# Agent attention: agents' scores laid out with pixels on partitions, half an image at a time, and two steps put on GpSimd

## The chip, the cores and the metric

The kernel runs on one core of one Trainium2 chip. The metric is the device time of one execution in microseconds (us); the median of three runs is quoted. Next to it stands one profiled execution, from which all durations of single instructions come.

## What is computed

The program is four residual layers, each `x = x + layer(groupnorm(x))`, on images of 32 x 192 x 56 x 56 in float32. The change touches layer 0 alone, an attention through 49 agents per head, six heads of 32 channels. Cut to what matters:

```python
qkv = xf @ Wqkv + bqkv                       # n = 3136 pixels, c = 192
agent = q averaged over 8 x 8 pixels         # A = 49 agents
agent_attn = softmax(ah * scale @ kh.T + pos_bias, axis=-1)    # over pixels
agent_v = agent_attn @ vh
q_attn = softmax(qh * scale @ ah.T + agent_bias, axis=-1)      # over agents
out = q_attn @ agent_v + depthwise3x3(v)
out = out @ proj_w + proj_b
```

The first softmax (the agents') has one row per head and agent, 294 rows of 3136 pixels. The second (the pixels') has one row of 49 for each pixel and head.

## The kernel before, in words

`attention` takes the 32 images one after the other (loop at line 833). An image is cut into four strips of columns, 16, 16, 16 and 8 wide (`WIDTHS`), each with its 56 rows in two halves; a strip holds 8 or 4 blocks of 112 pixels (`SUB`), 28 blocks in an image. `PAIR` is 98, two heads of 49 agents; `HA` is 294, all heads' agents. The keys and queries are never formed: `seen` (line 582 on) multiplies the agents into the weights, so that scores come straight from the normalised pixels `xs_a` and `xs_c` (which also carries the biases).

Agents' softmax, strip by strip. `weigh` (lines 651 to 667) makes scores with the agents on partitions: for each of three pairs of heads two halves of up to 448 pixels, each from two matmuls (lines 659, 660). VectorE finds the negated maximum straight from PSUM (line 661), ScalarE takes the exponential and the row's sum together (line 663). `turn` (line 682 on) transposes the weights on TensorE (line 691) so that pixels lie on partitions, ScalarE copies them to `prT` (line 694), and `gather` multiplies them with the transposed values (line 706). `settle` transposes the result back and adds two halves (lines 715 to 719). `join` (line 721 on) brings the four strips with their own maxima and sums together and gives `values`.

Pixels' softmax. `ask` (line 743 on) makes scores with pixels on partitions, 294 columns for each block (lines 751, 752), two blocks to a PSUM tile; VectorE finds the maximum of each head and subtracts it (lines 755, 756), ScalarE takes the exponential of four blocks (line 764), VectorE sums, inverts and multiplies (lines 766 to 768). `turn_back` transposes (line 778), `answer` multiplies with `values` and adds onto the convolution's result `o` (lines 791 to 797), `project` applies the last matrix and adds onto the image (lines 806 to 819).

Beside these stand the depthwise convolution of the values, `convolve` (eight multiply-adds on VectorE for each of two tiles, line 646; strip j needs the values of strip j + 1, which `find_v` makes), and `moments` (lines 507 to 536), the statistics and 8 x 8 sums of the next image.

The order. The program is written in a dataflow framework: it decides ahead of the run in which order each engine goes through its instructions, led by the order of writing and by what it reckons to be ready, and it puts in the waits. On the chip every engine then goes through its own list strictly in order. So the order of the calls in the loop (lines 841 to 887) is what one shapes. In the part before the loop over `t`, the four strips of the agents' softmax are written with the convolutions of the next strip between them; `moments` comes last, and `ask(0)` stands ahead of `join`. In the loop over `t` strips are asked, turned back, projected and answered in a staggered manner, and the next image's agents, values and first convolution are put between.

Buffers. All matmuls share four PSUM tiles of two banks (tag `ps`). `pr` and `pqT` share five SBUF buffers (tag `weights`), `prT` and `pq` two (tag `turned`).

## Time and profile before

| | us |
|---|---|
| median of 3 runs | 10793.86 (10781.03 to 10796.38) |
| the profiled execution | 10811.08 |
| its span, first to last instruction | 10809.3 |
| first agents' copy `gq_a` starts | 198.3 |
| last agents' copy `gq_a` starts | 4862.3 |
| TensorE clock granted, mean | 0.950 |

The attention is the first 45 per cent or so of the span; the scan of layer 1 follows, and the last part from about 8,370 us on does layers 2 and 3.

How to read the profile. PE is TensorE's matmuls and PEld its weight loads, DVE is VectorE, ACT ScalarE, POOL GpSimd, SP the engine that issues DMAs. A float32 matmul appears as two matmul instructions; a transpose as one. A line for a group of instructions gives: source line, engine, operation, what is written and read by the program's names, sizes as partitions x elements, the count; then busy us and mean ns of one; then how long the engine stood idle just before, and what ended that. A line for a stretch gives its bounds, its length, and then busy us of PE, PEld, DVE, ACT and POOL with the number of instructions, the granted clock and the DMA share. A line in order of time gives start, length, engine and instruction. The ends of matmuls are modelled: where matmuls follow each other, the distance of their starts is the price.

### The profile page before, as it was taken

The numbers are of one execution on the slowest core, as the hardware profiler recorded it, in microseconds if no ns is written. First come the engines' busy times: TensorE is split into PE (matmuls) and PEld (weight loads), VectorE is DVE, ScalarE is ACT, GpSimd is POOL, SyncE is SP. The second block draws the span as 40 slices with busy tenths as digits, with TensorE's granted clock in tenths as the row PEclk, the third lists the DMA queues.
The fourth block names the chain that finished last, engine by engine and source line by source line (L and its number), as shares of the span: only waits on it lengthen the run. The fifth ranks groups of instructions, "written<-read, shape, count | busy, mean of one in ns | idle before, by whom it ended". The sixth has DMA issues, their size and how long they took to land. (4 is left out here: it accounts for less than half of the span.)

```text
span 10809.3 us, 166766 instructions
## 1 busy us (share of the span) xinstructions
PE 9604.3 (89%) x64806; PEld 5959.0 (55%) x64806; DVE 9260.0 (86%) x11668; ACT 6372.8 (59%) x11964; POOL 2918.0 (27%) x2614
## 2 busy tenths in 40 slices
PE   6999999999999999998888888888888799999998
PEld 3555555555555555554333333333333577787876
DVE  5888888888888888887999999999999577777877
ACT  3555555555555555554666666666666466666766
POOL 0000000000000000002655555555555444444441
PEclk8999999999999999998999999999999899999999
DMA  4211221112121111111344333333444589999998
GB/s 122 63 47 49 63 64 63 37 58 63 64 63 35 61 46 46 46 34 56 92 102 98 97 97 97 97 97 97 97 101 103 153 269 273 274 275 273 278 274 264
DMA packets 1104877, 1240.31 MB, mean 115 GB/s; under 512 B 773091, under 2 KB 807200, under 8 KB 1091992
## 3 DMA queue, kind: packets, MB, share of 16 engines
q1 hardware_dynamic: 1083148, 1201.53, 38.8%
q10 hardware_dynamic: 20932, 28.02, 1.0%
q8 instruction: 516, 8.45, 0.3%
q14 instruction: 281, 2.30, 0.1%
HBM read 915.94 MB, written 306.43 MB: 113 GB/s over the span
## 5 line engine op out<-in xcount | busy, mean ns | idle before, releaser
L646 DVE SCALAR_TENSOR_TENSOR o<-v_a,att_w,o 128x896 f32<-128x896 f32 (+1 forms) x1024 | 1053.3, 1029 | 421.7 <-ACT v_a L620 296.6
L1163 POOL MEMSET f<- 128x1 f32 x96 | 8.8, 98 | 4842.7 <-DMA st_c<-st 4837.7
L1543 DVE STREAM_TRANSPOSE z<-turned 128x1792 f32<-128x1792 f32 x192 | 677.4, 3528 | 258.3 <-ACT turned L1543 257.8
L1543 ACT COPY y<-ps 64x252 f32<-64x252 f32 (+1 forms) x2304 | 784.0, 340 | 157.9 <-PE ps L1543 128.1
L1156 ACT ACTIVATE q<-q 128x784 f32<-128x784 f32 x384 | 328.3, 855 | 813.6 <-DVE q L1151 638.5
L663 ACT ACTIVATE pr<-ps,low 98x896 f32<-98x896 f32 (+1 forms) x384 | 352.3, 918 | 567.8 <-DVE low L661 567.8
L911 PE MATMUL ps<-sq,fixed 128*128 128x392 f32 x512 | 296.8, 742 | 427.7 <-ACT sq L1234 427.7
L764 ACT ACTIVATE pq<-pq 112x1176 f32<-112x1176 f32 x224 | 265.3, 1184 | 683.3 <-DVE pq L756 654.1
L751 PE MATMUL ps<-gq_a,xs_a 128*112 128x294 f32 x1792 | 609.0, 422 | 46.6 <-DVE pq L756 24.1
L1543 POOL TENSOR_TENSOR xn<-x,scale 128x896 f32<-128x896 f32 x192 | 328.4, 1711 | 1192.3 <-DMA x<-x 759.4
L646 DVE SCALAR_TENSOR_TENSOR o<-v_c,att_w,o 128x448 f32<-128x448 f32 (+1 forms) x1024 | 634.3, 619 | 7.5 <-ACT v_c L631 2.4
L659 PE MATMUL ps<-xs_a,gk_a 128*98 128x448 f32 (+1 forms) x1536 | 638.9, 497 | 0.0
L660 PE MATMUL ps<-xs_c,gk_c 125*98 125x448 f32 (+1 forms) x1536 | 631.3, 492 | 0.0
L911 PE MATMUL ps<-x,weights 128*128 128x392 f32 x1536 | 573.7, 516 | 31.1 <-DVE bv L1185 14.1
L752 PE MATMUL ps<-gq_c,xs_c 125*112 125x294 f32 x1792 | 581.4, 411 | 0.0
L1543 PEld LDWEIGHTS ps<-toep,y 128*32 128x32 f32 x16896 | 508.2, 151 | 113.4 <-ACT y L1543 109.2
L1543 PE MATMUL ps<-toep,y 128*32 128x112 f32 x16896 | 554.8, 287 | 0.0
L1543 PE MATMUL ps<-rows,xn 128*112 128x112 f32 x3072 | 378.5, 281 | 159.6 <-POOL xn L1543 136.0
L1543 ACT ACTIVATE turned<-ps,rs 128x448 f32<-128x448 f32 (+1 forms) x576 | 384.4, 668 | 203.4 <-PE ps L1543 195.7
L1543 PE MATMUL ps<-fixed,padded 128*128 128x168 f32 x3072 | 490.0, 314 | 0.0
L766 DVE TENSOR_REDUCE sm<-pq 112x24 f32<-112x1176 f32 x224 | 307.7, 1374 | 181.9 <-ACT pq L764 181.9
L1543 PEld LDWEIGHTS ps<-fixed,padded 128*128 128x128 f32 x3072 | 455.6, 195 | 2.4 <-issue 1.9
(367 smaller groups left out, 25548.6 us busy)
## 6 DMA issues: line engine op xcount, KB each, us to landing
toep<-spans SPq DMA_DIRECT2D x192, 2352.0 KB
x<-x SPq DMA_DIRECT2D x576, 392.0 KB
x<-x SPq DMA_DIRECT2D x896, 196.0 KB
out_x<-done SPq DMA_DIRECT2D x384, 196.0 KB
spans<-lags SPq DMA_DIRECT2D x24, 2352.0 KB
x<-in_x SPq DMA_DIRECT2D x32, 1568.0 KB
x<-x SPq DMA_DIRECT2D x32, 1568.0 KB
x<-in_x SPq DMA_DIRECT2D x64, 392.0 KB
```

Source lines behind the costliest of these rows:

```text
L646: nc.vector.scalar_tensor_tensor(dst, tap(i), dww[:, t, i : i + 1], dst, ALU.mult, ALU.add)
L659: mm(ps[P2, h, :n], g[:, cols], xs_a[j][:, px], start=True, stop=False)
L660: mm(ps[P2, h, :n], gk_c[0:KC, 2 * j + h, cols], xs_c[j][0:KC, px], start=False, stop=True)
L663: nc.scalar.activation(pr[:, :, :n], ps[P2, :, :n], AF.Exp, bias=low[:, j, p : p + 1], accum_out=sums[:, j, p : p + 1])
L751: mm(ps[:SUB, i, :HA], xs_a[j][:, px], g, start=True, stop=False)
L752: mm(ps[:SUB, i, :HA], xs_c[j][0:KC, px], gq_c[0:KC, 2 * j + (q + i) // ns], start=False, stop=True)
L764: nc.scalar.activation(flat, flat, AF.Exp)
L766: nc.vector.tensor_reduce(sm, rows, AX.X, ALU.add)
L911: mm(out, aa, srcs[t][h], start=True, stop=False)
L1156: nc.scalar.activation(den, den, AF.Ln)
L1163: nc.gpsimd.memset(s, 0.0)
L1543: return lambda *args, **kw: self.tc.keep_in_program_order(do(*args, **kw))
```

## The change

- `weigh` and `turn` go. `score` makes the agents' scores with pixels on partitions, in the form that `ask` has, and ScalarE copies them from PSUM to SBUF (`sc`, up to 8 blocks of 294).
- The softmax is kept for half images: strips 0 and 1, then strips 2 and 3. `highest` takes the maximum over the blocks on VectorE; `top` transposes these maxima, takes the maximum over the pixels and spreads the negated result over a diagonal matrix (`apart`); `lower` multiplies that with ones, which gives the row of maxima on all partitions, adds it to the scores on VectorE and takes the exponential on ScalarE. All are in place.
- `fold` adds the blocks up on GpSimd, and `add_up` finishes the sums with TensorE. `gather` and `settle` run once for each half image, and `join` has two parts to bring together in place of four.
- In `ask` the last product moves from VectorE to GpSimd.
- The block buffers become three of 8 blocks and one of 4. The tag `weights` has three buffers in place of five and also holds `by_x`, `tops`, `side` and `halves`. Some small tiles lose their second buffer.
- The calls of an image are written in a new order up to `join`; the loop over `t` stays.

```diff
--- before.py
+++ after.py
@@ -454,6 +454,7 @@
     mm = nc.tensor.matmul
     UP, LOW = slice(0, 64), slice(64, 128)
     HALVES = ((0, UP), (1, LOW))
+    WB = 3
...
@@ -473,6 +474,8 @@
     gk_c, gq_c, xs_c = ready.gk_c, ready.gq_c, ready.xs_c
 
     NK = len(WIDTHS)
+    ones = cp.tile([128, SUB], F32, name="ones", tag="ones")
+    nc.gpsimd.memset(ones, 1.0)
     xs_a = [cp.tile([128, S * w], F32, name=f"xs_a{j}", tag=f"xs_a{j}") for j, w in enumerate(WIDTHS)]
...
@@ -516,7 +519,7 @@
         nc.vector.bn_aggr(mv[:, 0], st_a.rearrange("p a b -> p (a b)"))
         nc.vector.bn_aggr(mv[:, 1], st_c.rearrange("p a b -> p (a b)"))
         pool_a, pool_c = small("pool_a", [128, AG]), small("pool_c", [65, AG])
-        by_x = [wp.tile([128, n, POOL], F32, name="by_x", tag=f"by_x{n}", bufs=1) for n in (S, S // 2)]
+        by_x = [wp.tile([128, n, POOL], F32, name="by_x", tag="weights", bufs=WB) for n in (S, S // 2)]
...
@@ -586,7 +589,7 @@
             n = (128, 65)[i]
             mm(ps[:n, i, : 4 * AG], w[0][:, cols], ag[0], start=True, stop=True)
             mm(ps[:n, i, 4 * AG : HA], w[1][:, cols], ag[1], start=True, stop=True)
-        g = small(name, [128, HA])
+        g = sp.tile([128, HA], F32, name=name, tag=name, bufs=1)
...
@@ -648,23 +651,74 @@
         return o
 
 
-    def weigh(j, g, low, sums):
-        _, n, _ = sizes(j)
-        prs = []
+    def blocks(j, name):
+        n = 2 * sizes(j)[2]
+        return wp.tile([SUB, n, HA], F32, name=name, tag=f"turned{n}", bufs=n // 4 + n // 8)
+
+    def score(j, g):
+
+        _, _, ns = sizes(j)
+        sc = blocks(j, "sc")
+        for q in range(0, 2 * ns, 2):
+            ps = psum()
+            for i in range(2):
+                px = slice((q + i) * SUB, (q + i + 1) * SUB)
+                mm(ps[:SUB, i, :HA], xs_a[j][:, px], g, start=True, stop=False)
+                mm(ps[:SUB, i, :HA], xs_c[j][0:KC, px], gk_c[0:KC, 2 * j + (q + i) // ns], start=False, stop=True)
+            nc.scalar.copy(sc[:, q : q + 2], ps[:SUB, :, :HA])
+        return sc
+
+    def highest(parts):
+
+        tops = wp.tile([SUB, 2, HA], F32, name="tops", tag="weights", bufs=WB)
+        for i, (j, sc) in enumerate(parts):
+            n = 2 * sizes(j)[2]
+            nc.vector.tensor_reduce(tops[:, i], sc[:, :n].rearrange("p q c -> p c q"), AX.X, ALU.max)
+        nc.vector.tensor_tensor(tops[:, 0], tops[:, 0], tops[:, 1], ALU.max)
+        return tops
+
+    def fold(parts):
+
+        (_, a), (j, b) = parts
+        side = wp.tile([SUB, 2, HA], F32, name="side", tag="weights", bufs=WB)
+        rest = [(t, q) for t, n in ((a, 8), (b, 2 * sizes(j)[2])) for q in range(0, n, 2)]
+        (t, q), (u, r) = rest[:2]
+        nc.gpsimd.tensor_tensor(side[:, 0:2], t[:, q : q + 2], u[:, r : r + 2], ALU.add)
+        for t, q in rest[2:]:
+            nc.gpsimd.tensor_tensor(side[:, 0:2], side[:, 0:2], t[:, q : q + 2], ALU.add)
+        nc.gpsimd.tensor_tensor(side[:, 0], side[:, 0], side[:, 1], ALU.add)
+        return side
+
+    def top(i, side, low):
+
+        ps = psum()
         for p in range(3):
-            cols = slice(p * PAIR, (p + 1) * PAIR)
-            ps = psum()
-            for h in range(2):
-                px = slice(h * n, (h + 1) * n)
-                mm(ps[P2, h, :n], g[:, cols], xs_a[j][:, px], start=True, stop=False)
-                mm(ps[P2, h, :n], gk_c[0:KC, 2 * j + h, cols], xs_c[j][0:KC, px], start=False, stop=True)
-            nc.vector.tensor_reduce(low[:, j, p : p + 1], ps[P2, :, :n], AX.XY, ALU.max, negate=True)
-            pr = wp.tile([PAIR, 2, CH], F32, name="pr", tag="weights", bufs=5)
-            nc.scalar.activation(
-                pr[:, :, :n], ps[P2, :, :n], AF.Exp, bias=low[:, j, p : p + 1], accum_out=sums[:, j, p : p + 1]
+            nc.tensor.transpose(ps[P2, 0, p * SUB : (p + 1) * SUB], side[:, 0, p * PAIR : (p + 1) * PAIR], ident[:SUB, :SUB])
+        nc.vector.tensor_reduce(
+            low[:, i], ps[P2, 0, : 3 * SUB].rearrange("p (a n) -> p a n", a=3), AX.X, ALU.max, negate=True
+        )
+        apart = sp.tile([PAIR, 3, PAIR], F32, name="apart", tag="apart", bufs=1)
+        nc.vector.tensor_tensor(
+            apart, ident[P2, P2].unsqueeze(1).to_broadcast([PAIR, 3, PAIR]), _bc(low[:, i], [PAIR, 3, PAIR]), ALU.mult
+        )
+        return apart
+
+    def lower(parts, apart):
+        ps = psum()
+        mm(ps[:SUB, 0, :HA], ones[P2, :SUB], apart.rearrange("p a b -> p (a b)"), start=True, stop=True)
+        for j, sc in parts:
+            n = 2 * sizes(j)[2]
+            nc.vector.tensor_tensor(
+                sc[:, :n], sc[:, :n], ps[:SUB, 0, :HA].unsqueeze(1).to_broadcast([SUB, n, HA]), ALU.add
             )
-            prs.append(pr)
-        return prs
+            flat = sc[:, :n].rearrange("p q c -> p (q c)")
+            nc.scalar.activation(flat, flat, AF.Exp)
+
+    def add_up(i, side, sums):
+        ps = psum()
+        for p in range(3):
+            mm(ps[P2, 0, p : p + 1], side[:, 0, p * PAIR : (p + 1) * PAIR], ones[:SUB, 0:1], start=True, stop=True)
+        nc.vector.tensor_copy(sums[:, i], ps[P2, 0, 0:3])
 
     def turn_v(j, v):
 
@@ -679,32 +733,20 @@
             nc.scalar.copy(vT[:, s0 : s0 + 2], ps[:SUB, :, : 3 * 128])
         return vT
 
-    def turn(j, prs):
-
-        _, _, ns = sizes(j)
-        prT = wp.tile([SUB, 8, HA], F32, name="prT", tag="turned", bufs=2)
-        for q in range(0, 2 * ns, 2):
-            ps = psum()
-            for i in range(2):
-                h, s = divmod(q + i, ns)
-                for p in range(3):
-                    nc.tensor.transpose(
-                        ps[:SUB, i, p * PAIR : (p + 1) * PAIR], prs[p][:, h, s * SUB : (s + 1) * SUB], ident[P2, P2]
-                    )
-            nc.scalar.copy(prT[:, q : q + 2], ps[:SUB, :, :HA])
-        return prT
-
-    def gather(j, prT, vT):
-
-        _, _, ns = sizes(j)
+    def gather(parts):
+
         ps = psum()
+        steps = [(s, sizes(j)[2], sc, vT) for j, sc, vT in parts for s in range(sizes(j)[2])]
         for p in range(3):
             cols = slice(p * PAIR, (p + 1) * PAIR)
-            for s in range(ns):
+            for k, (s, ns, sc, vT) in enumerate(steps):
                 for h, r in HALVES:
                     c = h * 128 + p * 64 if p < 2 else 256 + h * 64
-                    mm(ps[r, 0, cols], vT[:, s, c : c + 64], prT[:, h * ns + s, cols], start=(s == 0), stop=(s == ns - 1))
-        halves = wp.tile([128, HA], F32, name="halves", tag="halves", bufs=1)
+                    mm(
+                        ps[r, 0, cols], vT[:, s, c : c + 64], sc[:, h * ns + s, cols],
+                        start=(k == 0), stop=(k == len(steps) - 1),
+                    )
+        halves = wp.tile([128, HA], F32, name="halves", tag="weights", bufs=WB)
         nc.scalar.copy(halves, ps[:, 0, :HA])
         return halves
 
@@ -722,17 +764,17 @@
 
         m = small("m", [PAIR, 3])
         nc.vector.tensor_reduce(m, low.rearrange("p j a -> p a j"), AX.X, ALU.min)
-        f = small("f", [PAIR, NK, 3])
-        nc.vector.tensor_tensor(f, m.unsqueeze(1).to_broadcast([PAIR, NK, 3]), low, ALU.subtract)
+        f = small("f", [PAIR, 2, 3])
+        nc.vector.tensor_tensor(f, m.unsqueeze(1).to_broadcast([PAIR, 2, 3]), low, ALU.subtract)
         nc.scalar.activation(f, f, AF.Exp)
         nc.vector.tensor_tensor(sums, sums, f, ALU.mult)
         den = small("den", [PAIR, 3])
         nc.vector.tensor_reduce(den, sums.rearrange("p j a -> p a j"), AX.X, ALU.add)
         nc.vector.reciprocal(den, den)
-        nc.vector.tensor_tensor(f, f, den.unsqueeze(1).to_broadcast([PAIR, NK, 3]), ALU.mult)
+        nc.vector.tensor_tensor(f, f, den.unsqueeze(1).to_broadcast([PAIR, 2, 3]), ALU.mult)
         by_pair = got.rearrange("p j (a d) -> p (j a) d", a=3)
         nc.vector.tensor_tensor(
-            by_pair, by_pair, _bc(f.rearrange("p j a -> p (j a)"), [PAIR, NK * 3, 2 * HD]), ALU.mult
+            by_pair, by_pair, _bc(f.rearrange("p j a -> p (j a)"), [PAIR, 2 * 3, 2 * HD]), ALU.mult
         )
...
@@ -742,7 +784,7 @@
 
     def ask(j, g):
         _, _, ns = sizes(j)
-        pq = wp.tile([SUB, 8, HA], F32, name="pq", tag="turned", bufs=2)
+        pq = blocks(j, "pq")
...
@@ -765,7 +807,7 @@
             sm = sp.tile([SUB, 4 * HEADS], F32, name="sm", tag="sm", bufs=4)
             nc.vector.tensor_reduce(sm, rows, AX.X, ALU.add)
             nc.vector.reciprocal(sm, sm)
-            nc.vector.tensor_tensor(rows, rows, _bc(sm, [SUB, 4 * HEADS, AG]), ALU.mult)
+            nc.gpsimd.tensor_tensor(rows, rows, _bc(sm, [SUB, 4 * HEADS, AG]), ALU.mult)
...
@@ -778,7 +820,7 @@
                 nc.tensor.transpose(
                     ps[P2, h, s * SUB : (s + 1) * SUB], pq[:, q, p * PAIR : (p + 1) * PAIR], ident[:SUB, :SUB]
                 )
-            t = wp.tile([PAIR, 2, CH], F32, name="pqT", tag="weights", bufs=5)
+            t = wp.tile([PAIR, 2, CH], F32, name="pqT", tag="weights", bufs=WB)
             nc.scalar.copy(t[:, :, :n], ps[P2, :, :n])
...
@@ -828,35 +870,47 @@
     gk = seen(ag, wkT, gk_c, "gk_a")
     for j in range(NK):
         normed(nxt, rs, nb, j)
-    v, o = {0: find_v(0), 1: find_v(1)}, {}
-    o[0] = convolve(0)
+    v = {0: find_v(0), 1: find_v(1)}
+    o = {0: convolve(0)}
     for b in range(NB):
         x, more = nxt, b + 1 < NB
         if more:
             nxt = ready.image(nc, a, b + 1)
         beside(b)
-        low, sums = small("low", [PAIR, NK, 3]), small("sums", [PAIR, NK, 3])
-        got = sp.tile([PAIR, NK, C], F32, name="got", tag="got", bufs=1)
-        turned, asked, back = {}, {}, {}
-        for j in range(NK):
-            prs = weigh(j, gk, low, sums)
-            if j == 0:
-                gq = seen(ag, wqT, gq_c, "gq_a")
-            vT = turn_v(j, v[j])
-            if j > 0:
-                halves = gather(j - 1, *turned[j - 1])
-            if j + 2 < NK:
-                v[j + 2] = find_v(j + 2)
-            turned[j] = turn(j, prs), vT
-            if j > 0:
-                settle(j - 1, halves, got)
-            if j + 1 < NK:
-                o[j + 1] = convolve(j + 1)
-            elif more:
-                mv, pools = moments(nxt)
-        halves = gather(NK - 1, *turned[NK - 1])
+        low, sums = small("low", [PAIR, 2, 3]), small("sums", [PAIR, 2, 3])
+        got = sp.tile([PAIR, 2, C], F32, name="got", tag="got", bufs=1)
+        asked, back, sc, vT = {}, {}, {}, {}
+        sc[0] = score(0, gk)
+        gq = seen(ag, wqT, gq_c, "gq_a")
+        sc[1] = score(1, gk)
+        tops = highest([(j, sc[j]) for j in range(2)])
+        for j in range(2):
+            vT[j] = turn_v(j, v[j])
+        v[2] = find_v(2)
+        o[1] = convolve(1)
+        apart = top(0, tops, low)
+        sc[2] = score(2, gk)
+        lower([(j, sc[j]) for j in range(2)], apart)
+        v[3] = find_v(3)
+        o[2] = convolve(2)
+        sc[3] = score(3, gk)
+        side = fold([(j, sc[j]) for j in range(2)])
+        halves = gather([(j, sc[j], vT[j]) for j in range(2)])
+        add_up(0, side, sums)
+        tops = highest([(j, sc[j]) for j in range(2, 4)])
+        for j in range(2, 4):
+            vT[j] = turn_v(j, v[j])
+        settle(0, halves, got)
+        o[3] = convolve(3)
+        apart = top(1, tops, low)
         asked[0] = ask(0, gq)
-        settle(NK - 1, halves, got)
+        lower([(j, sc[j]) for j in range(2, 4)], apart)
+        if more:
+            mv, pools = moments(nxt)
+        side = fold([(j, sc[j]) for j in range(2, 4)])
+        halves = gather([(j, sc[j], vT[j]) for j in range(2, 4)])
+        add_up(1, side, sums)
+        settle(1, halves, got)
         values = join(low, sums, got)
         done, o = o, {}
         st = small("st", [128, 2, 9])
```

More of the change, by code (lines that the diff above doesn't have):

```diff
@@ L526, in moments @@
         )
-        fours = small("fours", [64, 2 * POOL, POOL])
+        fours = sp.tile([64, 2 * POOL, POOL], F32, name="fours", tag="fours", bufs=1)
         for h, r in HALVES:
```

## The prediction

> **What bounds the kernel now.** I read the page first (busy shares, slices), then the stretches of one image, then the groups of instructions in it, then single instructions in order of time.
>
> ```profile
> PE 9604.3 (89%) x64806; PEld 5959.0 (55%) x64806; DVE 9260.0 (86%) x11668; ACT 6372.8 (59%) x11964; POOL 2918.0 (27%) x2614
> ...
> PE   6999999999999999998888888888888799999998
> ...
> DVE  5888888888888888887999999999999577777877
> ...
> POOL 0000000000000000002655555555555444444441
> ```
>
> The change touches only the attention, slices 1 to 18 (to about 5,000 us). There GpSimd is idle, TensorE full and VectorE close to it. The copy of gq_a starts at 198.3 us in the first of the 32 images and at 4862.3 in the last: 150.5 us an image. Three stretches of one image (busy us of each engine follow the length):
>
> ```profile
> 2006.00:2070.00 64.00, 63.39 (x444) 40.91 (x443) 57.72 (x85) 36.54 (x74) 0.00 (x0) 1.00 0.37 124
> 2070.00:2098.00 28.00, 22.90 (x99) 16.55 (x97) 27.55 (x44) 6.04 (x8) 0.00 (x0) 0.88 0.00 1
> 2098.00:2157.50 59.50, 57.24 (x269) 31.32 (x268) 42.74 (x67) 38.55 (x64) 0.00 (x0) 0.97 0.05 11
> ```
>
> I call them A (agents' softmax, convolutions), B (moments of the next image, join, first pixels' softmax) and C (the other pixels' scores, answers, projection). The columns are PE, PEld, DVE, ACT, POOL. A is full on PE and DVE, B is full on DVE, C is PE's. So 92 us of the image have no room on VectorE (it works 85.3 of them), while C leaves it 17 us. Line 646, the depthwise taps, is 38.2 us of DVE's time in A, 0 in B, 11.2 in C by the same view for that line alone. The groups that the change touches or whose price I borrow (mean ns of one stands behind the bar):
>
> ```profile
> L646 DVE SCALAR_TENSOR_TENSOR o<-v_a,att_w,o 128x896 f32<-128x896 f32 x25 | 28.6, 1146 | 13.0 <-ACT v_a L620 9.3 <-ACT o L644 3.7
> L768 DVE TENSOR_TENSOR pq<-pq,sm 112x1176 f32<-112x1176 f32 x7 | 9.6, 1376 | 0.1
> L661 DVE TENSOR_REDUCE low<-ps 98x1 f32<-98x896 f32 x9 | 9.6, 1085 | 0.2 <-PE ps L660 0.2
> L738 DVE TENSOR_REDUCE values<-got 98x192 f32<-98x768 f32 x1 | 1.4, 1443 | 0.0
> ```
>
> **TensorE, per image.** The ends of matmuls are modelled, so I price by starts.
>
> ```profile
> 2101.47 0.66 PE L751 MATMUL ps<-gq_a,xs_a 128*112 128x294 f32 x2
> 2101.97 0.66 PE L752 MATMUL ps<-gq_c,xs_c 125*112 125x294 f32 x2
> ```
>
> Two 294-wide instructions per 0.50 us; a float32 matmul is two instructions. The new score has exactly this form: 28 blocks x 4 x 0.25 = 28.0. Weigh's pairs of 448 start 0.75 apart (36 pairs, 27.0) and its 224-wide ones cost half (12 pairs, 4.6): 31.6 go. Turn's 84 transposes go: 24 take 2.18 us in the timeline, so 7.6. Settle runs twice instead of four times: 6 transposes at 0.16, 1.0. Added: top, 6 transposes at 0.16, 1.0; lower, 4 instructions at 0.25, 1.0; add_up, 12 one-column instructions at 0.21 (line 542: 8 in 1.83), 2.5. Gather has as many matmuls as before. Sum: 32.5 against 40.2, about 8 us less.
>
> **ScalarE.** 14 copies of scores replace 14 copies of prT at the same 588 columns (659 ns). Three exponentials of 2352 and one of 1176 (1185 for 1176, slope 0.83 ns from line 663's two sizes) are 7.7 against 13.4 for line 663 with its accumulator reads. With the halved settle and halves about 7 us less. It is busy 81 of 151 us: worth nothing by itself.
>
> **VectorE, per image.** Highest reduces over blocks, so each step strides 1176 bytes. The nearest row is line 738, which also reduces across a stride: 1443 ns for 768 elements, 167 for line 724's 12, so 1.69 ns an element (lines 524 and 529, other strides, give about 1.7 too). 2352 elements: 4.1 us three times, 2.1 once, two 294-wide maxima at 0.45: 15.4. [...]
>
> Lower adds a PSUM row to SBUF scores, the form of line 793 (1076 for 896, 615 for 448): 2.6 us three times, 1.4 once, 9.1. Top: a 336-wide reduce (0.50, from line 661's 617 for 448) and a 294-wide product, twice: 1.9. Add_up's copies 0.2. That is 26.6 in 16 instructions; neighbours overlap some 0.08, so 25.3 added, all of it before or at the border of B. Removed there: line 661's 12 reduces, 10.5; two settles 0.5; half of join's two wide operations 1.2; three of the seven products of line 768, 3.6. Net +9.5 in A and B. The other four products leave C, about -5.5, where DVE is not the bound.
>
> **GpSimd.** A two-input operation of 896 takes 1.69 us there and one of 112 takes 0.42: 1.62 ns an element. Product of 1176: 2.14, seven times 15.0. Folds: 7 x 1.19 + 0.72 = 9.0 and 5 x 1.19 + 0.72 = 6.7. In all 31 us of an idle engine. [...] The row speaks for the move: in B DVE is full, so 3.6 us come free; and a turn_back follows the next ask in PE's queue (8 us of matmuls), which covers 0.8. I take 0 for the slower product, 5.4 if that cover is gone.
>
> But the two engines exclude one another when both read two operands from SBUF:
>
> ```profile
> 8990.94 1.61 DVE L1543 TENSOR_TENSOR apart<-total,fixed 128x32 f32<-128x32 f32 x1
> ```
>
> It takes 0.19 alone; here a GpSimd product runs from 8990.82 to 8992.51 and DVE ends with it, at 8992.55. Line 646 reads two SBUF operands; the reduces, line 793 and the new lower read one. Fold 0 comes beside convolve 2 and 3, where line 646 is 38.2/57.7 of DVE's work: about 6 of its 9 us are lost, less where GpSimd is the one that waits. Fold 1 comes beside moments (one operand), products beside ask: little. I take 5 us; ends 0 and 15.7 (both folds lost).
>
> **New waits.** Lower's matmul waits for apart, which sits in DVE's queue behind convolve 1 (13 us); behind it on PE stand find_v(3), score(3) and gather 0, and gather also waits for the exponentials. Highest 0 comes earlier than convolve 1 can, so it fills most of the 6.3 us that DVE stands idle in A (waits for v_a): I credit 4, ends 0 and 6. Three buffers of weights instead of five tie pqT, tops, side, halves and by_x together; answer frees them before the next turn_back, so 0, ends -0.5 and 3 an image. Ask 0 needs the block buffer of half 0, hence gather 0 and fold 0. No DMA is added or moved.
>
> **Sum.** A and B follow DVE: +9.5 + 5 - 4 = +10.5. PE's 8 us come off the same stretch, where they only become idle time: nothing of C can start there, because asks hold PSUM until DVE has reduced them. C: PE is 57.2 busy of 59.5, I take -1.5. Net +9 an image, 32 images: +288. The profiled execution took 10811.08 us (span 10809.3, 2 us around it), 17 above the median of 10793.86; on that median the forecast is 11,080.
>
> **Rivals.**
> - *Likeliest (0.50), 10,900 to 11,280, at 11,080:* VectorE's added passes lengthen A and B by what was summed.
> - *Late softmax (0.18):* as above, and PE runs out of other work before gather 0 and gather 1. Scores of half 0 take 16 us; highest's last part 5, top 1, convolve 1 in between 13, lower 5 and the last exponential 2 make 42, and fold's locks come on top. PE's work that needs no DVE is 28 of scores, 9 of v and 5 of transposes, 42 as well: no slack for half 0, and less for half 1. If each half leaves PE 4 us short beyond the forecast, 18 us an image, 11,370. For it: the queue above. Against: PE needs nothing more than 42.
> - *Faster (0.26):* taps drift behind the asks. C has 17 idle us on DVE and 5.5 freed. If some 14 of A's added 14.5 us (9.5 and the 5 of locks) run there, PE sets the image again: 151 - 8 = 143, with DVE at 128 + 9.5 - 5.5 + 5 = 137, tight, so I price -5 an image, 10,630 (10,500 to 10,770). It decides from where more than about 11 us drift. For it: o(2) and o(3) are not needed until their answers. Against: they are written ahead of the asks, and B had no line 646 at all.
> - *Cancels (0.04)* within 0.2%, 22 us, about what a measurement of this kernel tells from no change. The last 0.02 is a loss smaller than 10,900.
>
> **Numbers.** Faster 0.26, same 0.04, slower 0.70. The range runs from 10,620 (leaving about 0.09 of the faster case) to 11,420 (leaving about 0.08 of the late softmax). The likeliest case alone is 10,900 to 11,280.
>
> **What would show it.** [...] The forecast is wrong if line 646 is found in B and C in bulk and PE stays full, or if PE's largest wait is gather on exponentials.

## The result, and the profile after

The changed kernel takes 11930.28 us (median of 4 runs, 11921.08 to 11940.71), the kernel before, run beside it, 10795.12 (10781.03 to 10803.1): ratio 1.1053, 95% interval 1.1034 to 1.1073. That is 1135 us more, 35.5 us for each of the 32 images. The forecast had the sign right and 288 us; the time lies outside its range, which ended at 11,420.

The profile of the changed kernel, rows of busy time and of slices:

```profile
PE 9542.8 (80%) x63142; PEld 6087.7 (51%) x63142; DVE 9513.0 (80%) x11508; ACT 6228.1 (52%) x11196; POOL 4274.6 (36%) x3287
...
PE   5877778677786877877878888888888879999998
DVE  5777777777767777777779999999999968777777
```

In the attention (now slices 1 to 19) neither TensorE nor VectorE is full: they take turns in waiting. The period of the copy of `gq_a` is 185.4 us (196.1 us in the first image, 5943.4 in the last) instead of 150.5. An image is cut here into two stretches: from the first matmul of its scores to the first of ask 1, and from there to the next image's scores. The columns are those of the three stretches in the prediction. First the kernel before, cut in this way, then the changed kernel:

```profile
2006.00:2079.10 73.10, 71.48 (x476) 46.04 (x474) 66.42 (x103) 37.06 (x76) 0.00 (x0) 1.00 0.33 108
2079.10:2157.50 78.40, 72.06 (x332) 42.74 (x332) 61.59 (x92) 44.06 (x70) 0.00 (x0) 0.93 0.04 9
```

```profile
2428.40:2545.60 117.20, 72.64 (x424) 52.68 (x423) 86.30 (x110) 35.00 (x53) 31.90 (x16) 0.79 0.21 67
2545.60:2616.10 70.50, 68.40 (x334) 39.06 (x332) 49.25 (x80) 41.51 (x68) 10.88 (x5) 0.98 0.04 9
```

All of the loss lies in the first stretch. It is 44 us longer, with about the same work for TensorE, which idles 45 us in it; VectorE works 20 us more and still idles 31; the granted clock is 0.79 instead of 1.00. The second stretch is TensorE's and became 8 us shorter; VectorE idles 21 us in it. Over 18 images the first goes from 73.1 us to 116.5 on average, the second from 77.8 to 70.6.

What TensorE waited for, 1000 to 4500 us of the changed kernel, 18.9 images (total us, times, longest):

```profile
PE ps L720 <- POOL side L689: 347.5, 37, 14.3
PE ps L745 <- ACT sc L715: 210.9, 37, 9.6
PE ps L793 <- DVE low L697: 86.7, 19, 4.6
PE ps L696 <- DVE tops L677: 67.8, 19, 5.9
```

The same view of the kernel before has as its largest row:

```profile
PE ps L542 <- DVE pq L756: 58.6, 19, 3.1
```

So the largest new wait, 18.4 us an image, is that of the denominators' matmul (`add_up`, line 720) for the end of the fold on GpSimd (line 689). It is followed by `gather` (745) waiting for the exponentials (715), and by other links of the softmax chain, that is of the steps that follow one another in each half image: scores, maxima (`tops`), their spread (`low`, `apart`), the lowered scores, exponentials, `gather`.

The groups of VectorE and of GpSimd that the forecast had priced, changed kernel, 1000 to 5500 us, shapes kept apart:

```profile
L649 DVE SCALAR_TENSOR_TENSOR o<-v_a,att_w,o 128x896 f32<-128x896 f32 x576 | 670.0, 1163 | 217.9 <-ACT o L647 118.3 <-ACT v_a L623 98.7
...
L676 DVE TENSOR_REDUCE tops<-sc 112x294 f32<-112x2352 f32 x72 | 304.4, 4228 | 173.9 <-ACT sc L668 173.9
L711 DVE TENSOR_TENSOR sc<-sc,ps 112x2352 f32<-112x2352 f32 x73 | 187.7, 2604 | 0.0
...
L721 DVE COPY sums<-ps 98x3 f32<-98x3 f32 x48 | 7.7, 161 | 509.7 <-PE ps L720 509.7
```

```profile
L810 POOL TENSOR_TENSOR pq<-pq,sm 112x1176 f32<-112x1176 f32 x170 | 369.2, 2172 | 1727.9 <-DVE sm L809 1727.9
L688 POOL TENSOR_TENSOR side<-side,sc 112x588 f32<-112x588 f32 x244 | 350.3, 1436 | 17.5
L686 POOL TENSOR_TENSOR side<-sc 112x588 f32<-112x588 f32 x49 | 280.8, 5730 | 1725.6 <-ACT sc L715 1725.6
```

The prices hold: highest 4.23 us, lower 2.60, product 2.17. Line 721, a copy of three columns, is the new thing on VectorE: 0.16 us of work and 10.6 us of idle time ahead of each one, because it waits for line 720. And line 686, the first addition of each fold, is four times as long as line 688, which adds the same number of elements. One image in order of time shows both. GpSimd in fold 0 of the image whose `gq_a` copy stands at 2438.16:

```profile
2474.48 10.57 POOL L686 TENSOR_TENSOR side<-sc 112x588 f32<-112x588 f32 x1 [69.36 <-ACT sc L715]
2485.13 8.93 POOL L688 TENSOR_TENSOR side<-side,sc 112x588 f32<-112x588 f32 x6
2494.13 0.71 POOL L689 TENSOR_TENSOR side<-side 112x294 f32<-112x294 f32 x1
```

From 2472.04 to 2483.76 VectorE runs 14 taps of line 649 without a gap, each starting before the one ahead has ended. GpSimd's addition ends only after the last of them. Then TensorE, same image:

```profile
2494.89 1.16 PE L720 MATMUL ps<-ones,side 112*98 112x1 f32 x6 [14.32 <-POOL side L689]
2495.91 4.07 PE L732 MATMUL ps<-att_k,v 128*112 128x128 f32 x18
```

Behind line 720 stood 18 transposes of values (line 732) that needed nothing from the fold and waited with it. VectorE was idle from 2483.8 on for 12.3 us, since its next instruction, line 721, waits for this matmul; the maxima of half 1 (line 676) stand behind it:

```profile
2496.09 0.16 DVE L721 COPY sums<-ps 98x3 f32<-98x3 f32 x1 [12.32 <-PE ps L720]
2496.76 6.26 DVE L676 TENSOR_REDUCE tops<-sc 112x294 f32<-112x2352 f32 x2
```

### The profile page after: what moved, and what is told of

It reads as the page before. It is cut to its first block, busy times and chain, and to the rows that moved or that the text cites. A ratio compares the mean times of both kernels' runs of the same rounds, so it can differ in the third digit from the quotient of the medians.

```text
span 11924.0 us, 163854 instructions
## 1 busy us (share of the span) xinstructions
PE 9542.8 (80%) x63142; PEld 6087.7 (51%) x63142; DVE 9513.0 (80%) x11508; ACT 6228.1 (52%) x11196; POOL 4274.6 (36%) x3287
## 5 line engine op out<-in xcount | busy, mean ns | idle before, releaser
L810 POOL TENSOR_TENSOR pq<-pq,sm 112x1176 f32<-112x1176 f32 x224 | 486.5, 2172 | 2239.9 <-DVE sm L809 2231.5
L686 POOL TENSOR_TENSOR side<-sc 112x588 f32<-112x588 f32 x64 | 377.2, 5893 | 2297.3 <-ACT sc L715 2297.3
L793 PE MATMUL ps<-gq_a,xs_a 128*112 128x294 f32 x1792 | 679.7, 469 | 105.1 <-DVE low L697 104.8
L676 DVE TENSOR_REDUCE tops<-sc 112x294 f32<-112x2352 f32 (+1 forms) x128 | 471.5, 3708 | 224.6 <-ACT sc L668 224.6
L794 PE MATMUL ps<-gq_c,xs_c 125*112 125x294 f32 x1792 | 642.1, 449 | 0.0
L666 PE MATMUL ps<-gk_a,xs_a 128*112 128x294 f32 x1792 | 603.0, 418 | 0.0
L745 PE MATMUL ps<-sc,vT 112*64 112x98 f32 x5376 | 313.8, 282 | 348.8 <-ACT sc L715 346.3
L667 PE MATMUL ps<-gk_c,xs_c 125*112 125x294 f32 x1792 | 592.7, 412 | 0.0
L720 PE MATMUL ps<-ones,side 112*98 112x1 f32 x384 | 74.1, 308 | 616.9 <-POOL side L689 616.9
```

The costliest lines, as they stand in the source:

```text
L666: mm(ps[:SUB, i, :HA], xs_a[j][:, px], g, start=True, stop=False)
L667: mm(ps[:SUB, i, :HA], xs_c[j][0:KC, px], gk_c[0:KC, 2 * j + (q + i) // ns], start=False, stop=True)
L676: nc.vector.tensor_reduce(tops[:, i], sc[:, :n].rearrange("p q c -> p c q"), AX.X, ALU.max)
L686: nc.gpsimd.tensor_tensor(side[:, 0:2], t[:, q : q + 2], u[:, r : r + 2], ALU.add)
L745: mm(ps[r, 0, cols], vT[:, s, c : c + 64], sc[:, h * ns + s, cols], start=(k == 0), stop=(k == len(steps) - 1),)
L793: mm(ps[:SUB, i, :HA], xs_a[j][:, px], g, start=True, stop=False)
```

## The experiments

Letters in the expectations: Q is the theory that `add_up` stands wrongly in TensorE's queue; V, that VectorE has more to do than fits; T, that the place of the moments holds up the image's last stretch; P is told with its run. In the text, us an image are differences of medians over 32. The framework orders the lists of all engines anew for each run, so an edit can move more than the call that it names; where this matters it is said.

| run | median us | ratio to before [95%] |
|---|---|---|
| add_up of half 0 later | 11598.78 | 1.0735 [1.0717, 1.0753] |
| no fold | 11380.15 | 1.0533 [1.0515, 1.0551] |
| fold on VectorE | 11645.53 | 1.0778 [1.0760, 1.0796] |
| before + product on GpSimd | 10712.4 | 0.9912 [0.9895, 0.9928] |
| no fold, maxima of blocks | 11248.45 | 1.0418 [1.0400, 1.0435] |
| no fold, moments later | 11289.9 | 1.0461 [1.0444, 1.0479] |
| product alone, moments later | 10701.53 | 0.9917 [0.9900, 0.9933] |
| sums on TensorE | 11679.93 | 1.0812 [1.0794, 1.0830] |
| taps earlier | 11037.34 | 1.0233 [1.0205, 1.0262] |
| taps earlier, chain first | 10852.49 | 1.0057 [1.0034, 1.0081] |
| the same, with the fold | 10931.88 | 1.0132 [1.0104, 1.0160] |
| taps of convolve 3 at the end | 10990.79 | 1.0190 [1.0172, 1.0207] |
| order alone | 11042.51 | 1.0245 [1.0219, 1.0270] |
| taps of convolve 2 behind | 10987.02 | 1.0175 [1.0152, 1.0198] |
| taps of convolve 3 held at the end | 10858.61 | 1.0065 [1.0040, 1.0090] |
| TensorE kept busy | 11814.94 | 1.0952 [1.0929, 1.0976] |

**The fold's wait.** Three runs start from the changed kernel. In the first, one call moves:

```diff
         halves = gather([(j, sc[j], vT[j]) for j in range(2)])
-        add_up(0, side, sums)
...
         lower([(j, sc[j]) for j in range(2, 4)], apart)
         if more:
             mv, pools = moments(nxt)
+        add_up(0, side, sums)
```

> Everything of the changed kernel, but add_up of the first half image is called just ahead of the second fold instead of right behind the first gather. Theory Q (TensorE stands in its own queue in front of add_up until GpSimd has folded, 14.3 us for the first half and 5.0 for the second): the 14.3 go, about 14 us an image, 11,480. Theory V (VectorE's added passes set the image, as predicted): less than 2 us an image, 11,870 to 11,930.

11,599: 10.4 us an image come back, less than Q's full sum, and V's figure is excluded. VectorE's copy of the sums moved with the call, behind the maxima of half 1. The second leaves the fold out (`side = sc[0]` and `side = sc[2]`), so that the denominators are those of the first block of pixels alone:

> The fold on GpSimd is left out: add_up takes the sums over the first block of a half image alone, so the denominators are not the right ones; everything else stays. Theory Q: both waits go, 19 us an image, 11,310. Theory V: only the lock's loss on VectorE comes back, about 1 us an image, 11,900. If 35 us come back, fold alone is the whole loss.

11,380: 17.2 us an image, near the 19 of Q. But half of the loss is still there. The third does the fold on VectorE (`nc.vector` for `nc.gpsimd` in `fold`):

> The fold runs on VectorE instead of GpSimd, 12 sums of 588 at 0.76 us and two of 294 at 0.45, 10 us an image. Theory Q: the starved start (10.6 us for an operation of 1.4) goes, and VectorE stood idle for longer than the 10 us; 5 to 15 us an image are won, 11,450 to 11,770. Theory V: 10 us an image are lost, 12,250.

11,646: 8.9 us an image better, though VectorE has more to do; TensorE's largest wait is still this one:

```profile
PE ps L720 <- DVE side L689: 358.5, 39, 17.2
```

Over 19.8 images that is 18.1 us each, against 18.4: whichever engine folds, TensorE waits as long while the matmul stands there. The 8.9 us come together with another change: in this run VectorE's list has the maxima of half 1 ahead of the copy of the sums, and TensorE's waits for `tops` and `low` (lines 696 and 793; 67.8 and 86.7 us in the changed kernel) are gone.

**The product alone.** The kernel before with one word changed (`nc.gpsimd` in the last line of `ask`):

> The kernel before with one part of the change alone: the last product of the pixels' softmax on GpSimd. If VectorE bounds stretch B, as read in the profile: three products of 1.2 us come free, 3.6 us an image, 10,680. If the slower product (2.17 against 1.38 us) is waited for: up to 5.4 us an image lost, 10,970. Both small: within 30 us of before.

0.9912: 2.7 us an image gained, of the 3.6 that the forecast credited. The same with the moments at a later place (`moments` behind `ask(1)`):

> The kernel before with the product on GpSimd (10,712), and moments after ask 1. TensorE still idles some 4 us an image while VectorE is at moments, join and the first asks. Theory T: 2 to 4 us an image, 10,580 to 10,650. Against it: the next image's scaling waits for moments; then as much is lost, 10,780.

10,702 against 10,712, a difference too small to tell; these two are the quickest versions of all.

**What is left without the fold.** The waits of TensorE in the run without the fold:

```profile
PE ps L745 <- ACT sc L715: 191.2, 21, 9.9
PE ps L696 <- DVE tops L677: 155.3, 21, 9.0
```

With the two that follow (for `low` 83.7, for `apart` 77.4) they make about 25 us an image (20.5 images), all on the half images' chain: maxima, their spread, exponentials. Two runs ask whether VectorE's amount or the moments' place is behind it. Both leave the fold out as that run does. Maxima over adjoining blocks (steps of 588 columns) take the place of the strided reduction:

> The run without the fold (11,380; its denominators are not the right ones), and highest finds its maxima by adjoining blocks, operations of 588 at 0.68 us from start to start instead of reduces across a stride at 4.2: about 6 us less VectorE an image. Theory V (VectorE's work sets the first 90 us of an image): 6 us an image, 11,190. Theory L (it is the chain of waits, whose other links stay): the chain's first link is shorter by 2 to 3 us for each half, 11,220 as well; if neither, within 30 us of 11,380.

4.1 us an image, somewhat less than either theory had; a wait of 10.4 us for the maxima stays. Moments behind `ask(1)`:

> The run without the fold (11,380; denominators not the right ones), and moments of the next image (14 us of VectorE) is called after ask 1 instead of ahead of join. Theory T (the loss that is left is TensorE work, gather 1 and ask 1, pushed out of the stretch in which VectorE is full into the stretch that TensorE bounds): gather 1 and ask 1 come up to 14 us sooner, 8 to 12 us an image, 11,000 to 11,120. Theory V (the sum of VectorE's work): the same work at another place, within 60 us of 11,380.

2.8 us, short of T's 8 to 12: neither is the cause by itself. Then the true denominators without the fold, by one-column matmuls over all 28 blocks (with those maxima and late moments):

> The changed kernel with true denominators: no fold, add_up sums each block on TensorE (168 one-column instructions at 0.11 to 0.21 us, 18 to 35 us an image), highest by adjoining blocks, moments after ask 1. If both causes are taken away and TensorE's idle time takes the sums: 10,900 to 11,050. If TensorE bounds: up to 18 us an image more than that, 11,600.

11,680, above both figures: these matmuls (line 712, 3192 instructions, 421.0 us in 3500) take 22 us an image of TensorE, which is now busy 159 us of a period of 179.

**The order.** Two runs keep the maxima over blocks and still leave the fold out. First only the taps' place (theory P):

```diff
+        vT[0] = turn_v(0, v[0])
+        v[2] = find_v(2)
+        o[1] = convolve(1)
         sc[0] = score(0, gk)
...
         tops = highest([(j, sc[j]) for j in range(2)])
-        for j in range(2):
-            vT[j] = turn_v(j, v[j])
-        v[2] = find_v(2)
-        o[1] = convolve(1)
+        vT[1] = turn_v(1, v[1])
+        v[3] = find_v(3)
         apart = top(0, tops, low)
...
         lower([(j, sc[j]) for j in range(2)], apart)
-        v[3] = find_v(3)
         o[2] = convolve(2)
```

> The version without the fold and with the highest by maxima of adjoining blocks (11,248 us), with the VectorE work of the taps put at another place of the image: turn_v(0), find_v(2) and convolve(1) are written ahead of the first scores, turn_v(1) and find_v(3) behind the two reductions of the highest. As in the run it is built on, the denominators are those of the first block of pixels alone. Theory P (phase): what is left without the fold is that VectorE stands idle about 9 us at an image's start, waiting for scores, and TensorE later waits for VectorE; then this order gains 6 to 9 us an image, 10,960 to 11,060. Theory V (quantity: VectorE and TensorE together simply have more to do than they can lay beside each other): within 40 us of 11,248.

11,037: 6.6 us an image, as P expected. Then the chain of half 1 first:

```diff
-        o[3] = convolve(3)
         apart = top(1, tops, low)
-        asked[0] = ask(0, gq)
         lower([(j, sc[j]) for j in range(2, 4)], apart)
-        if more:
-            mv, pools = moments(nxt)
+        asked[0] = ask(0, gq)
+        o[3] = convolve(3)
...
         halves = gather([(j, sc[j], vT[j]) for j in range(2, 4)])
         add_up(1, side, sums)
+        if more:
+            mv, pools = moments(nxt)
```

> The version before it in this batch (taps moved ahead of the scores, no fold, denominators of the first block alone), with the softmax chain of half 1 put first: top 1 and lower 1 ahead of ask 0 and of the taps of convolve 3, the moments behind gather 1. If TensorE's wait for the exponentials in gather 1 is the doing of the written order, another 3 to 6 us an image less than that version (100 to 190 us); if the chain is as long as VectorE's queue makes it, within 40 us of it.

10,852: 5.8 us more, at the upper end. The wait of `gather` on the exponentials goes from 224.9 us of 3500 to 21.3:

```profile
PE ps L747 <- ACT sc L717: 21.3, 23, 1.1
```

Now the whole computation in this order:

> The version before it with the whole computation: the fold on GpSimd again, the denominators' matmuls of half 0 just ahead of the second fold, those of half 1 at the end of the image. If only the place of the denominators' matmuls in TensorE's queue made the fold dear, 3 to 6 us an image over that version (100 to 190 us); if the fold also costs by what it does beside VectorE, 10 us an image or more.

10,932: the fold costs 2.5 us an image here, somewhat less than the 3 to 6 expected, against 17.2 in the changed kernel. And the changed kernel with nothing but the order (strided reductions and all else as they were):

> The changed kernel (11,930 us) with nothing but its written order changed: the taps and value turns ahead of the scores, the chain of half 1 ahead of ask 0, the denominators' matmuls later, the moments behind gather 1; the reductions of the highest are those of the changed kernel. If the order alone explains the loss beyond the 4 us an image that the reductions cost as against maxima of adjoining blocks (132 us as measured without the fold), 11,030 to 11,100; if the reductions matter more or less when the order is mended, more than 11,150 or less than 10,980.

11,043, as expected: the order of the calls alone is worth 888 us, 27.7 of the 35.5 us an image.

**What remains** over the kernel before is 253 us with the strided reductions, 144 with the maxima. In the version with the fold TensorE's largest wait is that for the maxima of half 1:

```profile
PE ps L698 <- DVE tops L679: 232.9, 23, 10.1
```

The taps of `convolve(3)` were to go into the loop over `t`, where VectorE has room (called in two pieces, at t = 2 and t = 3):

> The whole computation in the order of the last run of the batch before (10,932 us), with one thing moved: the taps of convolve 3 (eight of about 1.16 us and eight of about 0.69 us on VectorE) leave the first half of the image, where VectorE is full and TensorE waits about 10 us for the maxima of half 1, and stand in two pieces in the loop of the last stretch (after the turns t = 2 and t = 3), where VectorE idles about 18 us. If what is left is VectorE being full in one half of the image and idle in the other, 5 to 10 us an image less: 10,610 to 10,770, at or below the kernel before; if the taps only delay the reductions of the ask and the next image's start, 10,900 or more.

A miss: 59 us slower. The price in the expectation was wrong too: strip 3 is half as wide, its taps take 0.68 and 0.44 us. And they had not moved. In VectorE's order of time they run at the old place, between and ahead of the steps of the maxima, where the framework had put them back; TensorE's wait for the maxima stays, with up to 11.6 us.

Before this was seen, the next run moved `convolve(2)` behind `ask(0)` in the text:

> The run before it (10,991 us, the taps of convolve 3 in the last stretch) with the taps of convolve 2 moved from ahead of the reductions of half 1 to behind lower 1 and ask 0. In that run TensorE still waited 11.6 us an image for the maxima of half 1, with taps standing between VectorE's reductions of half 0 and of half 1. If those taps are what holds the maxima, the wait falls to about 3 us and the image by 5 to 9 us: 10,700 to 10,830, the kernel before's time or less. If VectorE is simply full there, the wait comes back at gather 1 or at the ask: 10,900 or more.

The framework made of it the very same instruction lists on all engines, so it is a repetition (10,987 against 10,991). The last of these holds the taps of strip 3 by their data:

```diff
+        late = small("late", [128, 2])
+        nc.vector.scalar_tensor_tensor(
+            late, halves[:, 0:1].to_broadcast([128, 2]), 0.0, dwb[:, 0:2], ALU.mult, ALU.add
+        )
         settle(1, halves, got)
...
-                done[3] = convolve(3, (0,))
+                done[3] = convolve(3, (0,), late)
```

> The whole computation as in the run with the taps of convolve 3 in the last stretch (10,991 us), with those taps held there by their data: their bias is made from the result of gather 1 times zero plus the bias (one small operation on VectorE), so that they can't be run earlier. In that run the framework had put them back, ahead of and between the steps of the maxima of half 1 (all eight of 0.68 us and eight of 0.44 us, 9 us alone, more beside the fold), and TensorE waited 11.6 us an image for those maxima. If the taps in front are what keeps TensorE waiting there, the wait falls to about 3 us and the image by 5 to 9 us: 10,700 to 10,830. If the next image's statistics and the chain itself hold the maxima, or the taps now delay the asks, 10,900 or more.

10,859, between the two figures: 4.1 us an image better than with the taps put back, 65 us over the kernel before. The wait for the maxima shrinks to 7.7 us (177.3 in 3500 instead of 265.4).

In the image looked at, the six steps of the maxima now follow the next image's statistics (7 us), and the fold's additions take 1.57 us on average (1.44 in the changed kernel). So the place of the taps accounts for part of the rest. Holding back the statistics too was not tried, so how much of the last 65 us is place and how much the fold's presence stays open.

**The clock.** In the changed kernel TensorE's busy time does not fall by the 8 us of work that were saved. Taken without overlaps from the trace, between the 7th and the 25th copy of `gq_a`, it is 142.8 us an image before, 141.1 after, and 134.8 in the run with the order alone, which issues the same matmuls. The stretches around the 14.32 us wait show TensorE's clock there (changed kernel; first the last matmuls ahead of the wait; in the lines of stretches the third figure from the end is the granted clock):

```profile
2477.80 2.78 PE L745 MATMUL ps<-sc,vT 112*64 112x98 f32 x62
```

```profile
2480.00:2484.00 4.00, 0.57 (x14) 0.38 (x10) 3.77 (x5) 0.41 (x1) 4.00 (x1) 0.86 0.00 0
2484.00:2488.00 4.00, 0.00 (x0) 0.00 (x0) 0.00 (x0) 0.00 (x0) 3.84 (x3) 0.50 0.00 0
...
2495.00:2498.00 3.00, 3.00 (x16) 3.00 (x17) 1.91 (x3) 0.54 (x1) 0.00 (x0) 0.50 0.00 0
2498.00:2501.00 3.00, 2.36 (x13) 2.10 (x11) 3.00 (x2) 2.04 (x4) 0.00 (x0) 0.67 0.00 0
```

The clock is at half within 4 us of the last matmul, and still at half while TensorE works again. Ask 0, just behind another wait, issues its pairs 0.98 us apart instead of 0.50. In this image VectorE comes to ask 0's scores only at 2521.57, from other work and without waiting, so there the slow matmuls held nobody up. One more run, on the changed kernel, adds matmuls that nobody uses and takes nothing away:

```diff
     def add_up(i, side, sums, sc):
         ps = psum()
+        for k in range((22, 6)[i]):
+            mm(ps[:SUB, 1, :HA], sc[:, 0, :SUB], sc[:, k % 4], start=True, stop=True)
```

> The changed kernel (11,930 us) with work added that nobody uses: 22 matmuls of 294 columns (44 instructions of 0.25 us, 11 us) ahead of the denominators' matmuls of half 0 and 6 (3 us) ahead of those of half 1, where TensorE waits 14.3 and 5.0 us for the fold. In the trace of the changed kernel the granted clock falls to 0.50 in that wait and the matmuls behind it run at half speed for about 5 us; TensorE's busy time an image is 141 us there and 135 where the waits are gone. If that lowered clock is on the path, the run is faster in spite of the added work, by 1 to 3 us an image (11,830 to 11,900), and the clock of the attention rises; if the half-speed matmuls lie beside VectorE's work, the time stays within 25 us of 11,930; slower would mean that the added work itself comes to stand in the way.

11,815: 115 us, 3.6 us an image faster with 14 us an image of work added, more than the 1 to 3 expected. The granted clock from 1000 to 4500 us is 0.90 instead of 0.86, and ask 0's pairs stand 0.50 apart. But this does not show that the clock made it faster. TensorE's list is the old one plus these matmuls, but for two neighbours changed over in 7 images, while VectorE's list is another one: in all 32 images the framework has put the maxima of half 1 ahead of the copy that waits for the denominators (here line 723), and so into what was idle time:

```profile
2454.24 4.18 DVE L676 TENSOR_REDUCE tops<-sc 112x294 f32<-112x2352 f32 x1
...
2472.00 0.16 DVE L723 COPY sums<-ps 98x3 f32<-98x3 f32 x1 [9.31 <-PE ps L722]
```

These are about 7 us of VectorE's work. TensorE's wait for `tops` (67.8 us in 3500) is gone and that for `low` is down from 86.7 to 21.4. This may account for the whole gain. So it is shown that TensorE worked at half speed behind these waits (0.50 granted, pairs 0.98 us apart for 0.50) and was busy 6 us an image more for the same matmuls (141.1 against 134.8); what that adds to the time beyond the waits themselves stays open.

In stretches of 0.25 us the trace has the granted clock at 1.00 up to 2482.75, 0.78 in the next and 0.50 from 2483.00 on; behind the wait at 0.50 up to 2499.75, 0.58 in the next and 1.00 from 2500.00 on. So here it fell at about 2482.9, 2.3 us after the last matmul had ended (2480.58), and rose at about 2500.0, 5.1 us after work had begun again (2494.89).

## Why the prediction was wrong, step by step

- **Prices of instructions: right.** Highest 4.23 us (4.1 forecast), lower 2.60 (2.6), product 2.17 (2.14). The 5.4 us an image set down for a slower product that is waited for (seven times 2.14 less 1.38) did not show: the product alone gained 2.7 us an image. The fold's additions took 1.44 instead of 1.19. VectorE's busy time an image went from 128.0 to 136.0, +8.0; the forecast had +9.5 in A and B, -5.5 in C and +5 for the exclusion of the two engines, +9.0.
- **"New waits": the step that failed.** It went through lower, gather, the weights and ask 0, and left out `add_up`, the one matmul that waits for the fold, which so was put at nothing. "31 us of an idle engine" is true and beside the point: what the idle engine makes is awaited in order by TensorE, with 18 transposes behind it, and by VectorE's copy of the sums behind that. The wait took 18.4 us an image; without the fold 17.2 us come back. Where the forecast had +10.5 us for A and B, the stretch from an image's first scores to ask 1, which is nearly these two, grew by 43.4.
- **Late softmax, the other half of the loss, was a rival with 0.18.** It had the right mechanism: gather waits for exponentials 11.2 us an image (210.9 over 18.9). It had the low chance because TensorE's independent work just reached ("42 as well: no slack"); an order with no slack should have been the likelier case. Its size, 18 us (its own terms, 9 and twice 4, make 17), is near what is left without the fold, 18.3 (585 us over 32). That is in part luck: of the 25 us of waits in that run only 9 are gather's.
- **TensorE's 8 us: right as work, not found in the changed kernel.** 142.8 to 134.8 where the waits are mended, but 141.1 in the changed kernel. "Only become idle time" left out the clock: in the first stretch, where TensorE idles 45 us, it was 0.79 on average, against 1.00 before.
- **Exclusion, 5 us on VectorE: the wrong loser.** What the kernel before shows of it, 8600 to 10,600 us: of 42 instructions `apart<-total,fixed` (both operands in SBUF, 0.19 us alone) that start while GpSimd runs a two-operand instruction, 40 end 0.04 to 0.05 us behind it, after up to 1.72 us; 90 reductions (`sums<-sq`, 1.08) and 71 additions with an operand in PSUM (`x<-x,ps`, 0.62) took there what they take alone (1.07 and 0.62). In the changed kernel the 896-wide taps went from 1146 to 1163 ns and the 448-wide ones from 678 to 697, under 1 us an image. It was GpSimd that waited, 10.57 us for an addition of 1.4. With the taps of convolve 3 at the end VectorE does lose: behind the lowered scores of half 0, where the fold stands, taps took up to 1.84 us for 0.67 and a step of the maxima 1.27 for 0.76. The forecast said "less where GpSimd is the one that waits" and then asked only what VectorE loses, not who waits for GpSimd.
- **"C: I take -1.5": right in direction.** From ask 1 to the next image's scores it is 7.2 us shorter. VectorE has 12 us less to do there (61.6 to 49.3): cut in this way all seven products (9.6 us) stood in it, and some of ask 0's reductions now lie ahead of it.
- **The -4 us of filled idle time: came, and went again.** The taps' wait for `v_a` fell from 9.2 us an image to 4.1, but VectorE now waits for scores at the image's start (line 676: 173.9 us, 7.2 an image). Writing the taps ahead of the scores gave 6.6 us an image.
- **Faster is excluded.** The taps did not drift: VectorE spends 11.2 us on 12 of them behind ask 1, before and after, and idles 21 us there.

The sum itself, +9, was the price of quantities in an order without new waits. The run with only the order changed is at +253 us, 7.9 an image. That the two figures are near is no proof of the terms; but it says where the 35.5 came from: 27.7 from where calls stand.

## What to carry to other kernels

When a step moves to an idle engine, look for the instruction that consumes its result and list what stands behind it in its engine's queue: here one tiny matmul held TensorE 18 us an image, and the same fold cost 2.5 once that matmul stood elsewhere. When a change turns one stream (strip by strip) into two phases (all maxima, then all exponentials), count the work that can fill the gap at each phase border before summing durations. When TensorE waits for several us, look at the granted clock of what follows, and price the matmuls behind the wait by it (here 0.98 us a pair for 0.50). And compare the lists of all engines before an effect is put down to an edit: matmuls that nobody uses, put on TensorE, changed the order of VectorE's work.

## What the runs showed of the hardware that was not expected

- An addition on GpSimd stood 10.57 us behind a train of VectorE's two-operand instructions that overlapped at their ends; the train lost almost nothing (1163 for 1146 ns). In the run with the taps of convolve 3 at the end, where VectorE's list has statistics among the taps there, VectorE lost: taps took up to 1.84 us for 0.67, a step of the maxima 1.27 for 0.76.
- Around the 14.32 us wait TensorE's granted clock fell from 1.00 to 0.50 about 2.3 us after the last matmul and stayed there for the first 5.1 us of the work that followed; TensorE was busy 141.1 us an image with the waits and 134.8 without them, for the same matmuls.
- Moving a two-input product to GpSimd (2.17 us for 1.37 on VectorE) gained 0.9% in the kernel before, where VectorE worked 27.55 us of the 28 us of stretch B and GpSimd had nothing to do in the attention.
